# Packing two heads or row blocks into the TensorE array, folding one layer's weights, and fixing the issue order in three attention layers

## The chip, the cores and the metric

The kernel runs on one core of a Trainium2 chip. The metric is the device time of one execution in microseconds (us), median of several runs on the same chip. Each kernel is compared with runs of before from its own rounds. Where two changed kernels are compared below, their medians can come from different jobs and chips; before's median was 5836.9 to 5843.3 us there, so such differences are good to some 6 us.

## The reference, cut to what matters

Four layers follow each other on two images of 512 channels and 32 x 32 = 1024 pixels, all in fp32. Layer 0 (a deformable attention with a position bias, then an MLP) is the longest and is not changed. Layers 1 to 3 are attention over 1024 pixels:

```python
# layer 1: group norm, 8 heads of 64 channels, projection, residual
w = softmax(einsum('bct,bcs->bts', q * scale, k * scale));  hh = einsum('bts,bcs->bct', w, v)
x = x + proj_w @ hh
# layer 2: group norm, one head of 512 channels, projection, residual
attn = softmax(einsum('bci,bcj->bij', q, k) * C ** -0.5);   out = einsum('bcj,bij->bci', v, attn)
x = x + w_proj @ out
# layer 3: q and k have 64 channels, softmax over the queries, residual
attn = softmax(einsum('bdi,bdj->bij', q, k), axis=1);       x = gamma * einsum('bci,bij->bcj', v, attn) + x
```

## The kernel before

Every attention goes through one helper. It takes 128 rows of one head at a time: scores into PSUM, row maximum, exponential, division by the sum, eight transposes, two copies out of PSUM; after four such row blocks the values are multiplied. The emission order is only a proposal: the framework's scheduler sets the order of instructions on each engine.

```python
    def attend(qk, scale, vT, chunks, store):
        for tb in range(2):
            pT = [ptp.tile([P, 4, HALF], F32, name="pT", tag="pT") for _ in range(2)]
            for t4 in range(4):
                rows = slice(tb * HALF + t4 * P, tb * HALF + (t4 + 1) * P)
                sc = ps_s.tile([P, HW], F32, name="score")
                for half in range(2):
                    n = slice(half * HALF, (half + 1) * HALF)
                    for i, (q, k) in enumerate(qk):
                        nc.tensor.matmul(sc[:, n], q[:, rows], k[:, n], start=(i == 0), stop=(i == len(qk) - 1))
                nm = small.tile([P, 1], F32, name="nm")
                nc.vector.tensor_reduce(nm, sc, AX.X, ALU.max)
                nc.vector.tensor_scalar(nm, nm, -scale, None, ALU.mult)
                p = pp_.tile([P, HW], F32, name="p")
                sm = small.tile([P, 1], F32, name="den")
                nc.scalar.activation(p, sc, AF.Exp, bias=nm, scale=scale, accum_out=sm)
                nc.vector.reciprocal(sm, sm)
                nc.gpsimd.tensor_scalar(p, p, sm, 1.0, ALU.mult, ALU.mult)
                # ... eight transposes into two PSUM tiles tp; VectorE copies one to pT, ScalarE the other
            # ... values: for each chunk of channels, 8 matmuls of vT against pT, 512 columns wide

    for b in range(B):  # layer 1: eight heads of 64 channels
        # ... group norm, projections q, k, values vT
        for head in range(8):
            m, r = head // 2, slice(head % 2 * 64, head % 2 * 64 + 64)
            # ...
            attend([(q[m][r], k[m][r])], 64 ** -0.5, vT, [(head * 64, 64)], store)
        add_projection(x, proj1, "proj_b", o)
```

A score matmul of layer 1 uses 64 of the 128 rows of the TensorE array, a value matmul 64 of its 128 columns. PSUM holds two score tiles of two banks each, two `tp` tiles, and two tiles for all other products.

## Time and profile before

The median was 5840.04 us of three runs (5839.96 to 5842.33). The stages of the profiled run, from the first starts of their matmuls:

| stage | from (us) | to (us) | length |
|---|---|---|---|
| layer 0 with its MLP | 0 | 4182 | 4182 |
| layer 1, two images | 4182 | 5068 | 886 |
| layer 2, two images | 5068 | 5553 | 485 |
| layer 3, two images | 5553 | 5837 | 284 |

The page's first part gives each engine's busy time, its share of the span and its number of instructions:

```profile
PE 5147.2 (88%) x14146; PEld 1848.4 (32%) x14146; DVE 2487.8 (43%) x2868; ACT 1559.0 (27%) x1820; POOL 1469.3 (25%) x804
```

PE is TensorE, PEld its weight loads, DVE VectorE, ACT ScalarE, POOL GpSimd.

### The profile page before, as it was taken

To read this page: it belongs to the slowest core of one execution; us is meant where nothing else is said; L and a number is where in the kernel's file an instruction comes from. 1 tells how busy PE (TensorE), PEld (TensorE's weight loads), DVE (VectorE), ACT (ScalarE), POOL (GpSimd) and SP (SyncE) were. 2 spreads that over 40 slices of the span, in tenths; PEclk is the share of its full clock that TensorE was granted. 3 is DMA by queue.
4 is the path that set the end of the run, shared out by engine and by line. 5 is a ranking of instruction groups with operands and counts; after the bars stand their busy time and mean duration, and the time that the engine had idled before them with its cause. 6 is when DMAs were issued, how large, how long until landed. Compare 5 with 4: busy or idle time off the path is not lost.

```text
span 5837.3 us, 35881 instructions
## 1 busy us (share of the span) xinstructions
PE 5147.2 (88%) x14146; PEld 1848.4 (32%) x14146; DVE 2487.8 (43%) x2868; ACT 1559.0 (27%) x1820; POOL 1469.3 (25%) x804
## 2 busy tenths in 40 slices
PE   3788888888888888888888888899999999999999
PEld 1222222222222222222222222344444444444444
DVE  6455555555555455555555555200034334311121
ACT  3233333333333233333333333100123223210111
POOL 1233333333333233333333333100012112100000
PEclk7999999999999999999999999999989989999988
DMA  2100000000000000000000000000100000000000
GB/s 91 37 15 8 8 15 8 9 14 8 12 10 8 8 15 8 7 15 8 8 15 8 8 15 0 29 0 0 58 0 1 0 0 1 9 0 0 0 13 17
DMA packets 51416, 70.36 MB, mean 12 GB/s; under 512 B 7072, under 2 KB 40240, under 8 KB 50608
## 3 DMA queue, kind: packets, MB, share of 16 engines
q1 hardware_dynamic: 48992, 63.09, 4.1%
q10 hardware_dynamic: 2256, 4.98, 0.2%
q8 instruction: 112, 1.84, 0.1%
q14 instruction: 56, 0.46, 0.0%
HBM read 63.59 MB, written 4.46 MB: 12 GB/s over the span
## 4 chain that ended last, share of the span: by engine, by line
PE 62%; DVE 20%; ACT 9%; POOL 4%; DMA 4%; issue 2%; ACTq 0%; POOLq 0%; SPq 0%; DVEq 0%
PE z L318 18%; DVE h L320 9%; ACT h L314 8%; DVE h L307 8%; PE pav L531 8%; PE sim L325 7%; PE score L507 7%; PE pm L478 4%; PE ph L395 4%; PE pp L402 4%; DMA tab<-slog_d 3%; PE tp L520 3%; PE pmv L488 3%; POOL h L307 3%; PE ppr L542 2%
## 5 line engine op out<-in xcount | busy, mean ns | idle before, releaser
L318 PE MATMUL z<-h,cpb_w 128*128 128x512 f32 x4096 | 1983.0, 614 | 492.4 <-ACT h L314 492.4
L320 DVE TENSOR_SCALAR h<-z,pc 128x1024 f32<-128x1024 f32 x1024 | 1311.2, 1280 | 1549.4 <-PE z L318 1549.2
L314 ACT ACTIVATE h<-h 128x1024 f32<-128x1024 f32 x1024 | 1082.0, 1057 | 2363.1 <-DVE h L307 1852.2
L307 POOL TENSOR_TENSOR h<-tab,tab 128x1024 f32<-128x1024 f32 x512 | 1161.8, 2269 | 2090.9 <-PE z L318 2090.8
L318 PEld LDWEIGHTS z<-h,cpb_w 128*128 128x128 f32 x4096 | 696.6, 189 | 1806.2 <-ACT h L314 1106.9
L325 PE MATMUL sim<-h,w 128*32 128x512 f32 x4096 | 1033.1, 603 | 3.7 <-DVE h L320 3.7
L307 DVE TENSOR_TENSOR h<-tab,tab 128x1024 f32<-128x1024 f32 x512 | 625.3, 1221 | 13.9 <-POOL tab L299 13.9
L515 POOL TENSOR_SCALAR p<-p,den 128x1024 f32<-128x1024 f32 x160 | 178.7, 1117 | 1271.8 <-DVE den L514 1078.6
L531 PE MATMUL pav<-pT,vT 128*64 128x512 f32 (+1 forms) x1024 | 462.0, 609 | 0.2 <-DVE pT L525 0.2
L507 PE MATMUL score<-qk 64*128 64x512 f32 (+1 forms) x832 | 424.4, 655 | 7.4 <-ACT p L513 7.0
L325 PEld LDWEIGHTS sim<-h,w 128*32 128x32 f32 x4096 | 169.1, 108 | 748.0 <-issue 545.0
L509 DVE TENSOR_REDUCE nm<-score 128x1 f32<-128x1024 f32 x160 | 195.6, 1222 | 174.9 <-PE score L507 174.9
L531 PEld LDWEIGHTS pav<-pT,vT 128*64 128x64 f32 (+1 forms) x1024 | 169.1, 168 | 289.0 <-issue 286.1
L513 ACT ACTIVATE p<-score,nm 128x1024 f32<-128x1024 f32 x160 | 178.5, 1116 | 264.0 <-DVE nm L510 264.0
L520 PE MATMUL tp<-cst,p 128*128 128x128 f32 x1280 | 192.9, 299 | 33.1 <-POOL p L515 33.1
L395 PE MATMUL ph<-xn,wa 128*128 128x512 f32 x512 | 220.5, 592 | 1.1 <-POOL xn L388 1.1
L402 PE MATMUL pp<-hid,wb 128*128 128x512 f32 x512 | 220.4, 592 | 0.0
L523 ACT COPY pT<-tp 128x512 f32<-128x512 f32 x160 | 93.3, 583 | 451.0 <-PE tp L520 451.0
L520 PEld LDWEIGHTS tp<-cst,p 128*128 128x128 f32 x1280 | 152.1, 151 | 165.0 <-POOL p L515 93.9
L491 DVE TENSOR_TENSOR vT<-pmv,vbias 128x512 f32<-128x512 f32 x48 | 33.2, 691 | 398.5 <-PE pmv L488 398.5
L507 PEld LDWEIGHTS score<-qk 64*128 64x128 f32 (+1 forms) x832 | 145.4, 199 | 174.6 <-issue 137.6
L405 DVE SCALAR_TENSOR_TENSOR x<-pp,pc,x 128x512 f32<-128x512 f32 x16 | 12.0, 750 | 416.1 <-PE pp L402 416.1
(135 smaller groups left out, 2030.6 us busy)
## 6 DMA issues: line engine op xcount, KB each, us to landing
tab<-slog_d SPq DMA_DIRECT2D x64, 512.0 KB, 7.5
xt<-in_xt ACTq DMA_DIRECT2D x4, 1024.0 KB, 9.5
x<-in_x SPq DMA_DIRECT2D x8, 512.0 KB, 10.6
wa<-in_mlp_w SPq DMA_DIRECT2D x4, 1024.0 KB, 8.5
wb<-in_mlp_w SPq DMA_DIRECT2D x16, 256.0 KB, 5.3
out<-x SPq DMA_DIRECT2D x16, 256.0 KB, 2.0
wa<-in_qkv_w SPq DMA_DIRECT2D x4, 768.0 KB, 7.7
wb<-in_qkv_w SPq DMA_DIRECT2D x4, 768.0 KB, 6.4
```

The costliest lines, as they stand in the source:

```text
L307: eng.tensor_tensor(h1, tabs[0][:, quad, ri, :].unsqueeze(1).to_broadcast([P, H, W]), tabs[1][:, quad, ri, :].unsqueeze(2).to_broadcast([P ...
L314: nc.scalar.activation(h1f, h1f, AF.Relu)
L318: nc.tensor.matmul(z[:, n], cpb_w2, h1f[:, n], start=True, stop=True)
L320: nc.vector.tensor_scalar(h2, z, col("cpb_b2"), 0.0, ALU.add, ALU.max)
L325: nc.tensor.matmul(sim[quad * 32 : quad * 32 + 32, n], w3[:, 31 - r : 63 - r], h2s[quad][:, n], start=False, stop=(r == 31),)
L395: nc.tensor.matmul(ph, w1[:, k, m * P : (m + 1) * P], xn[:, k, :], start=(k == 0), stop=(k == CC - 1))
L402: nc.tensor.matmul(pp, w2[:, k, m * P : (m + 1) * P], h1[:, k, :], start=(k == 0), stop=(k == HID // P - 1))
L478: nc.tensor.matmul(pm[:rows], w[:, k, cols], h[k][:, n], start=(k == 0), stop=(k == CC - 1))
L507: nc.tensor.matmul(sc[:, n], q[:, rows], k[:, n], start=(i == 0), stop=(i == len(qk) - 1))
L509: nc.vector.tensor_reduce(nm, sc, AX.X, ALU.max)
L520: nc.tensor.transpose(tp[:, i, :], p[:, s * P : (s + 1) * P], ident)
L531: nc.tensor.matmul(pm[:n], vT[:, s, lo : lo + n], pT[s // 4][:, s % 4, :], start=(s == 0), stop=(s == 7))
```

## The change

The change wants TensorE to do less, and to fix the order by hand so that the packing holds:

- layer 1: two heads of a channel chunk share the array, in the scores by rows, in the values by columns; the values come in blocks of 256 rows;
- layer 2: `q'k = h' (Wq'Wk) h` and `Wproj (Wv h) = (Wproj Wv) h`, so two products of weights are made on chip once, and an image needs neither a key nor an output projection;
- layer 3: two row blocks share the array in the scores, and the projections of q and k are written twice side by side;
- everything after the MLP keeps the order of emission on each engine (`in_order`), with each pass's transposes and values one or two passes behind its scores, and projections and group norms cut into steps between them.

```diff
+@contextmanager
+def in_order(tc):
+    # ... collects the instructions emitted inside
+        if i.engine in before:
+            tc.add_manual_dep(i, before[i.engine], ..., reason="in_order")
+        before[i.engine] = i.name
...
+    def softmax(sc):
+        nm = small.tile([P, 1], F32, name="nm", tag="nm", bufs=4)
+        nc.vector.tensor_reduce(nm, sc, AX.X, ALU.max, negate=True)
+        p = pp_.tile([P, HW], F32, name="p")
+        sm = small.tile([P, 1], F32, name="den", tag="den", bufs=4)
+        nc.scalar.activation(p, sc, AF.Exp, bias=nm, accum_out=sm)
+        nc.vector.reciprocal(sm, sm)
+        nc.gpsimd.tensor_scalar(p, p, sm, 1.0, ALU.mult, ALU.mult)
+        return p
...
+    def scores1(qk, rb):
+        # ...
+        for half in range(2):
+            n = slice(half * HALF, (half + 1) * HALF)
+            for head in range(2):
+                r = slice(head * 64, head * 64 + 64)
+                nc.tensor.matmul(sc[head][:, n], q[r, rows], k[r, n], start=True, stop=True)
+        return [softmax(s) for s in sc]
...
+        for s in range(8):                       # values, weigh1
+            for head in range(2):
+                nc.tensor.matmul(pm[head * 64 : head * 64 + 64], vT[:, s, lo : lo + 64], pTs[head][:, s, :], ...)
...
+        for i in range(32):                      # layer 1, one image
+            m, rb = divmod(i, 8)
+            ps = scores1(qk, rb)
+            # ... on some passes one step of the next pair's projection, or of a group norm
+            # ... then the transposes of pass i - 1, both heads
+            if i % 2 and i >= 3:
+                weigh1(vT, o, (i - 3) // 8, (i - 3) // 2 % 4, block_T.pop((i - 3) // 2))
```

The diff is cut to its core; names and order are as in the kernel.

## The prediction

> **What bounds the kernel now.** I read the page first, then busy time by stretch, then the timeline, then single records. Layers 1 to 3 run from 4182 to 5837 us. The order of instructions on each engine is the same in both programs up to the end of the MLP (only one load is gone), so about 4182 us cannot move, and all is decided in 1655 us. The windows view (start and end, length, then busy time of each engine, and the granted clock) of layer 1's attention of one image, of layer 2's and of layer 3's:
>
> ```profile
> core 0: us, PE busy (x) PEld busy (x) DVE busy (x) ACT busy (x) POOL busy (x), PEclk, DMA share, GB/s
> 4273.00:4597.00 324.00, 312.82 (x1024) 133.40 (x1024) 142.54 (x273) 113.49 (x194) 71.52 (x64) 0.95 0.00 1
> 5160.00:5283.00 123.00, 118.77 (x319) 55.26 (x318) 23.07 (x40) 16.88 (x26) 8.93 (x8) 0.99 0.00 0
> 5595.00:5695.00 100.00, 94.98 (x229) 43.83 (x229) 22.96 (x41) 13.73 (x24) 8.94 (x8) 0.85 0.05 19
> ```
>
> TensorE is the bound in all three, at 95 to 97%, with VectorE below half. So fewer TensorE passes should help, as long as something else does not start to wait. The clock of 0.85 in layer 3 says that time is lost there in another way. The timeline shows both the packing and the clock:
>
> ```profile
> 2003.04 1.90 PE L325 MATMUL sim<-h,w 128*32 128x512 f32 x10
> ...
> 4300.77 3.78 PE L507 MATMUL score<-qk 64*128 64x512 f32 x4
> ...
> 4313.21 1.09 PE L520 MATMUL tp<-cst,p 128*128 128x128 f32 x8
> 4314.23 1.12 PE L507 MATMUL score<-qk 64*128 64x512 f32 x2
> 4316.31 1.13 PE L507 MATMUL score<-qk 64*128 64x512 f32 x4
> 4323.19 1.98 PE L507 MATMUL score<-qk 64*128 64x512 f32 x4
> ```
>
> An fp32 matmul is two records, 429 ns apart at 512 columns. Two score records take 1.12 us, and four on both halves of the rows take 1.13 us: two heads already share the array here by chance, while four alone take 1.98 us. The sim line does the same with column strips, ten records in 1.90 us. So packing works at nearly the full factor, for rows and for columns. At 4300 us the same four records take 3.78 us: the clock is at half from 4277 to 4308 us, although TensorE has no gap there.
>
> **What the skill says.** "TensorE: Matmul & The Clock Gate", Part 1, has a free-running activity window of 3413 ns after which the clock goes from full to half or back. The trace agrees: the records of the clock hold 0.5 for multiples of 3.41 us. From the starts of the matmuls I worked out each window's share of activity, counting a lone 64-row matmul as half. Over some 1,600 windows the clock fell only where the share was at most 0.36 and rose only where it was 0.75 or more. Part 4 of that page has transposes not counting as busy; here windows with 0.16 of scores and 0.50 of transposes kept the full clock, so I count them. "TensorEngine Tiling (Array Packing)", section PSUM Bottleneck, warns that packing speeds TensorE and not what empties PSUM. No stage before is limited so; this is where I expect it. The same page's Key Properties have a drain when the tiling mode changes: 520 ns to the next start where the form changes, against 429.
>
> **The change part by part.** Units: a 512-column fp32 matmul is 0.857 us, four plus four transposes 0.9 to 1.0 us.
>
> Layer 2: the keys' and the output's projection vanish, 32 + 32 matmuls an image, 2 x 64 x 0.857 = 110 us. In their place come 48 transposes and 32 matmuls once (some 10 + 27 us), 32 products with one column (about 8 us from the group norm's pairs of 0.39 us), and a wait of 8 us for layer 2's weights: they can be loaded only when the MLP has let go of the slot at 4181, and landed by 4191 before. So 54 us of it come back. The group norm goes beside matmuls, 2 x 8 us. Attention: scores 8 x 6.96, transposes 8 x 1.0, values 4 x 13.9 (256 columns, 214 ns each) = 119 us for 123 now, still TensorE bound. A layer 2 image costs 27 + 27 + 119 = 174 instead of 243 us.
>
> Layer 1: packed scores save half of 256 matmuls in two images, packed values another half of 256: 256 x 0.857 = 219 us of TensorE work. Will it be time? One pass of the loop takes two heads' 128 rows. The durations of its chain, from the page:
>
> ```profile
> L509 DVE TENSOR_REDUCE nm<-score 128x1 f32<-128x1024 f32 x160 | 195.6, 1222 | 174.9 <-PE score L507 174.9
> L513 ACT ACTIVATE p<-score,nm 128x1024 f32<-128x1024 f32 x160 | 178.5, 1116 | 264.0 <-DVE nm L510 264.0
> L525 DVE COPY pT<-tp 128x512 f32<-128x512 f32 x160 | 109.7, 685 | 85.4 <-PE tp L520 84.1
> L523 ACT COPY pT<-tp 128x512 f32<-128x512 f32 x160 | 93.3, 583 | 451.0 <-PE tp L520 451.0
> ```
>
> The fixed order makes VectorE do: maximum of head A, reciprocal A, maximum B, reciprocal B, then the two copies of the rows before. The built program shows exactly this. A reciprocal waits for its exponential, so VectorE stands still twice. From the first score: scores 1.98; hop 0.09; then twice maximum 1.22, hop 0.12, exponential to reciprocal 1.24 (median of the records), reciprocal 0.1: 7.4 us; copy 0.7: 8.1. The second head's eight transposes need the two PSUM buffers that this copy and ScalarE's empty, so they run 8.2 to 9.2. Only then come the values (every second pass, 16 packed pairs of 214 ns, 3.6 us with the switches) and the next scores. Even passes 9.2, odd 12.8: 22.0 us a pair, while TensorE's own work is some 14. An image has 16 pairs: 352, less 6 for the first pair, plus 12 for group norm work that sits on VectorE inside this chain: 358 us against 324 now. The next pair's projections (24 of the 32 steps an image) hide in the waits, 3.4 us each.
>
> The clock: in an odd pass TensorE idles from 2.8 to 8.2 us. A hole of 5.4 us holds a window below 0.35 at any phase, so the clock halves, and the second head's transposes and the values start cold. Depending on phase it comes back 3 to 6 us after work resumes, half of which is lost: 2.1 us. A projection shortens the hole to about 2 us, a share of 0.38, just safe. Without projection are four of eight passes for three head pairs and all eight of the last: (3 x 4 + 8) x 2.1 = 43 us an image. So the attention loop is 401 us for an image where it was 324.
>
> Layer 3: scores packed, but the same chain: first pass 7.4, then three of 9.2 + 13.9, last 2.3 + 13.9, cold starts about 8: 101 us, and 41 for projections and values: 143 an image against 142.
>
> Sum in us from the start: MLP end 4182; fold 54, first q and k 14, values 27: 4277; image 0 401, next image's q and k sticking out 9, tail 6: 4693; values and projection 55: 4748; image 1 401, layer 2's product 27, tail 4: 5180; values and projection 55: 5235; layer 2 174 + 120: 5529; layer 3 286: 5815; last store and launch edges some 6: 5821. I say 5825.
>
> **Rivals.** First, packing pays in full: if VectorE's chain hid behind TensorE, layer 1 loses 219, layer 2 some 70 net, and the time is about 5550. For it speaks that TensorE was 97% busy and VectorE 44% in the layer 1 stretch; against it the fixed order, in which nothing of VectorE's can move ahead of a reciprocal that waits. Second, the chain holds but the clock stays up (packed matmuls counting more, or the hole being shorter): 2 x 43 + 2 x 8 less, about 5720. Third, the clock also falls in the passes with a projection, whose share of 0.38 is close to 0.36: 24 passes of up to 2.1 us, and longer cold stretches feed on themselves: 5870 to 5920. Fourth, matmuls of 256 columns might wait for their weights (190 ns a load against 214 ns of streaming): at 20 ns each over the some 1,000 such records of layers 2 and 3, 20 us more.
>
> **Range and chances.** The part outside layer 1 is arithmetic on measured durations, good to 20 us. The chain is good to 0.5 us in 64 passes, 32 us; the clock's share may be 0 to twice 100. That gives 5740 to 5915. Under 5723 needs the chain and the clock both milder than reckoned, over 5957 needs cold passes nearly throughout; that such a rewrite is meant to gain adds a little to faster.
>
> **What would show it.** After: in layer 1 a stretch of loop near 400 us an image, TensorE busy about 75%, waits of the transposes on VectorE's or ScalarE's copies as TensorE's longest, the maximum's idle time ended by reciprocals and exponentials, the eight score records of a pass in about 2 us, mean clock near 0.85 there and near 1 in layer 2, each layer 2 loop near 120 us. I am wrong if the loop takes under 330 us, if the waits of the transposes are short, or if packed pairs run one after the other.

## More of the kernel before

What counts for the change is what TensorE waits for inside layer 1's attention. The waits of TensorE, from 4273 to 4597 us (who waited for whom: us in total, times, longest):

```profile
PE tp L520 <- POOL p L515: 8.4, 9, 3.3
PE score L507 <- ACT p L513: 2.4, 1, 2.4
```

These are 11 of 324 us: the scheduler had interleaved the heads so well that TensorE almost never stood still.

## The result, and the profile after

The changed kernel takes 5818.28 us (5813.74 to 5821.17, four runs) against 5840.0 of before: a ratio of 0.9963, 95% interval 0.9949 to 0.9977. Ratios are the mean time of one kernel's fast runs over that of the other's of the same rounds, so they are not quite the ratios of the medians quoted. The results are correct. The page has TensorE busy 247 us less:

```profile
PE 4900.4 (84%) x15154; PEld 1930.7 (33%) x15154; DVE 2459.4 (42%) x2736; ACT 1571.5 (27%) x1848; POOL 1472.3 (25%) x804
```

The stages against the prediction's sum, in the profiled run of 5819 us:

| stage | before | predicted | measured |
|---|---|---|---|
| end of the MLP to the first layer 1 score | 91 | 95 | 109 |
| layer 1 loop, image 0, with what sticks out | 324 | 416 | 408 |
| layer 1 loop, image 1, with layer 2's first product | 323 | 432 | 425 |
| layer 2, image 0, with the next image's products | 243 | 174 | 182 |
| layer 2, image 1 | 242 | 120 | 118 |
| layer 3, two images | 284 | 286 | 285 |

The columns do not cut the work in the same places (projections moved into the loops), so the first column shows only the scale. The windows view of the changed kernel, for layer 1's loop of image 0, layer 2's loop of image 1 and layer 3's of image 0; the columns are those of the prediction's first fence:

```profile
4291.00:4699.00 408.00, 293.89 (x1412) 164.54 (x1412) 141.97 (x234) 125.81 (x213) 76.54 (x68) 0.83 0.00 1
...
5417.00:5534.00 117.00, 116.65 (x446) 79.03 (x445) 23.12 (x39) 13.98 (x25) 8.97 (x8) 1.00 0.00 0
5576.00:5675.00 99.00, 81.94 (x352) 64.29 (x352) 30.50 (x54) 14.59 (x25) 8.97 (x8) 0.88 0.06 21
```

In layer 1 TensorE is now busy 294 of 408 us, 72% where it was 97%, and at a mean clock of 0.83. Layer 2's loop of image 1 has no holes. A pass is the work on one block of 128 rows of two heads; each head pair has eight. The timeline of TensorE for two passes of layer 1, the second cut, after the values of the pass before:

```profile
4377.99 3.67 PE L647 MATMUL pav<-pT,vT 128*64 128x256 f32 x32
4381.60 1.99 PE L638 MATMUL score<-k,q 64*128 64x512 f32 x8
4383.51 1.09 PE L544 MATMUL tp<-cst,p 128*128 128x128 f32 x8
4389.40 1.94 PE L544 MATMUL tp<-cst,p 128*128 128x128 f32 x8 [4.79 <-ACT pT L547]
4391.26 3.79 PE L638 MATMUL score<-k,q 64*128 64x512 f32 x8
...
4400.86 1.94 PE L544 MATMUL tp<-cst,p 128*128 128x128 f32 x8 [4.49 <-ACT pT L547]
4402.73 5.21 PE L647 MATMUL pav<-pT,vT 128*64 128x256 f32 x32
```

The eight score records of two heads take 1.99 us, as four of one head did before, and 32 value records 3.67 us: the packing works. But the second eight transposes of a pass wait 4.5 to 4.8 us for a copy, and what follows such a hole runs at half clock: transposes 1.94 instead of 1.09, scores 3.79 instead of 1.99, values 5.21 instead of 3.67. VectorE in the pass that starts at 4381.60 shows where the wait comes from:

```profile
4383.61 1.23 DVE L530 TENSOR_REDUCE nm<-score 128x1 f32<-128x1024 f32 x1 [1.42 <-PE score L638]
4386.17 0.16 DVE L534 RECIPROCAL den<-den 128x1 f32<-128x1 f32 x1 [1.33 <-ACT p L533]
4386.25 1.22 DVE L530 TENSOR_REDUCE nm<-score 128x1 f32<-128x1024 f32 x1
4388.81 0.16 DVE L534 RECIPROCAL den<-den 128x1 f32<-128x1 f32 x1 [1.33 <-ACT p L533]
4388.89 0.67 DVE L549 COPY pT<-tp 128x512 f32<-128x512 f32 x1
```

Both reciprocals end a stop of 1.33 us in which VectorE waits for an exponential. The transposed rows of the first head have lain in PSUM since 4384.6, and the copy that frees a buffer starts at 4388.89. ScalarE's copy stands behind the second exponential, and so behind the same reciprocal; in this pass it freed the first buffer, and most of the waiting ends with it. TensorE's waits in the same loop:

```profile
PE tp L544 <- ACT pT L547: 74.8, 16, 6.3
PE tp L544 <- DVE pT L549: 24.6, 17, 1.9
```

The transposes wait 99 us for copies where before they waited 8.4 us for GpSimd. A hole also costs through the clock, which the next section takes apart.

### The profile page after: what moved, and what is told of

Its sections match the earlier page's. It is cut to its first block, busy times and chain, and to the rows that moved or that the text cites. A ratio compares the mean times of both kernels' runs of the same rounds, so it can differ in the third digit from the quotient of the medians.

```text
span 5819.4 us, 37975 instructions
## 1 busy us (share of the span) xinstructions
PE 4900.4 (84%) x15154; PEld 1930.7 (33%) x15154; DVE 2459.4 (42%) x2736; ACT 1571.5 (27%) x1848; POOL 1472.3 (25%) x804
## 4 chain that ended last, share of the span: by engine, by line
PE 55%; DVE 20%; ACT 11%; POOL 5%; DMA 3%; issue 2%; ACTq 0%; POOLq 0%; SPq 0%; DVEq 0%
PE z L337 18%; DVE h L339 9%; ACT h L333 8%; DVE h L326 8%; PE sim L344 7%; PE pav L505 4%; PE ph L415 4%; PE pp L422 4%; DMA tab<-slog_d 3%; PE pmv L505 3%; POOL h L326 3%; PE pav L647 3%; PE score L638 3%; ACT p L533 2%; PE tp L544 2%
## 5 line engine op out<-in xcount | busy, mean ns | idle before, releaser
L544 PE MATMUL tp<-cst,p 128*128 128x128 f32 x1280 | 219.2, 326 | 241.1 <-ACT pT L547 180.5
L544 PEld LDWEIGHTS tp<-cst,p 128*128 128x128 f32 x1280 | 178.5, 169 | 319.4 <-issue 280.6
L505 PE MATMUL pav<-pT,vT 128*128 128x256 f32 x1024 | 233.5, 390 | 1.5 <-DVE pT L549 1.5
L505 PEld LDWEIGHTS pav<-pT,vT 128*128 128x128 f32 x1024 | 199.6, 196 | 32.5 <-DVE pT L549 3.7
L638 PE MATMUL score<-k,q 64*128 64x512 f32 x512 | 154.4, 714 | 8.5 <-ACT p L533 8.5
L549 DVE COPY pT<-tp 128x512 f32<-128x512 f32 x160 | 108.4, 681 | 108.1 <-PE tp L544 107.5
L647 PE MATMUL pav<-pT,vT 128*64 128x256 f32 x1024 | 150.4, 458 | 0.0
```

Source lines behind the costliest of these rows:

```text
L505: nc.tensor.matmul(pm, w, m, start=(k == 0), stop=(k == len(pairs) - 1))
L544: nc.tensor.transpose(tp[:, i, :], p[:, s * P : (s + 1) * P], ident)
L638: nc.tensor.matmul(sc[head][:, n], q[r, rows], k[r, n], start=True, stop=True)
L647: nc.tensor.matmul(pm[head * 64 : head * 64 + 64], vT[:, s, lo : lo + 64], pTs[head][:, s, :], start=(s == 0), stop=(s == 7),)
```

## The experiments

The theory: the fixed order makes a pass of layer 1 as long as VectorE's chain, and the clock falls in the hole that this leaves on TensorE. The rivals: TensorE's work is still what counts; the packing is worth less than it seems; the clock does not matter. All experiments gave correct results; each was run three rounds against before.

**Late reciprocals.** In layers 1 and 3 the maxima of both heads come first, the reciprocals after the copies.

```diff
-        return [softmax(s) for s in sc]
+        return [softmax_a(s) for s in sc]        # maximum, exponential
...
                 for head in range(2):
                     transposed(...)
+                for s_ in ps:
+                    softmax_b(*s_)                # reciprocal, division
```

> In layers 1 and 3 the two maxima come first on VectorE, then the copies of the transposed rows, and only then the two reciprocals; no work is added or removed. If VectorE's fixed order with its two stops at the exponentials sets the length of a pass (my theory), the second head's transposes can start 1.7 us earlier: a pair of passes goes from 22.0 to about 18.8 us, 32 pairs give 100 us, some 40 us of cold clock and 15 us of layer 3 go with it: about 5660 us (5630 to 5700). If TensorE's own work or the packing is what holds (rival), nothing changes: 5818 within 15 us.

Measured: 5645.33 us, ratio 0.967 (0.9655 to 0.9684). Moving the two reciprocals of a pass, 0.16 us each, and the divisions on GpSimd behind them, without adding or removing work, gave 173 us; in the profiled runs 153 us of it lie between layer 1's first score and layer 2's, and 24 in layer 3. VectorE in a pass of layer 1:

```profile
4369.79 2.35 DVE L530 TENSOR_REDUCE nm<-score 128x1 f32<-128x1024 f32 x2 [3.65 <-PE score L647]
4372.06 0.68 DVE L558 COPY pT<-tp 128x512 f32<-128x512 f32 x1
4373.55 0.69 DVE L558 COPY pT<-tp 128x512 f32<-128x512 f32 x1 [0.81 <-PE tp L553]
4374.16 0.21 DVE L538 RECIPROCAL den<-den 128x1 f32<-128x1 f32 x2
```

The first copy starts 2.3 us after the first maximum, where it was 5.3 us. Passes without values went from 9.1 to 7.9 us. The order of VectorE was what set the pass; the rival falls.

**Serial scores.** The loops over heads and halves are exchanged, so that one head's scores are issued before the other's.

```diff
-        for half in range(2):
-            # ... n of this half
-            for head in range(2):
+        for head in range(2):
+            # ... r of this head
+            for half in range(2):
                 # ...
                 nc.tensor.matmul(sc[head][:, n], q[r, rows], k[r, n], start=True, stop=True)
```

> In layer 1 the scores of the two heads are no longer issued alternately but one head after the other, so they cannot share the array: 64 passes, each with 1.71 us more of TensorE time. If the pass is set by VectorE's chain (my theory), this hides in the hole of TensorE: within 25 us of the changed kernel, 5800 to 5845 us, and the clock falls less often, as the hole is shorter. If packing the scores is worth its TensorE time (rival), 64 x 1.71 = 110 us are lost: about 5925 us.

Measured: 5813.86 us, ratio 0.9959 (0.9944 to 0.9974), as the theory expected, but the run proves nothing. Its timeline shows that the scores stayed packed:

```profile
4408.36 1.99 PE L638 MATMUL score<-k,q 64*128 64x512 f32 x8
```

The built program has two matmuls of one head and then two of the other; in the trace the eight records start in four pairs, 13 or 14 ns apart. Taken in the program's order, the second head's first record could not start before the first head's fourth, over 1.2 us later.

**Filling with matmuls.** Four matmuls into a spare PSUM tile that nobody reads, in every layer 1 pass that has no projection step.

```diff
+            if (m == 3 or rb in (0, 1, 3, 5)) and not (b == 0 and i == 31):
+                fill()      # 4 matmuls of 512 columns
```

> Four 512-column matmuls of 3.4 us, whose result nobody reads, are put into the hole of every layer 1 pass that has no projection in it, 46 passes in two images, some 158 us of pure waste on TensorE. If the hole is idle anyway and costs twice because the clock falls in it (my theory), the clock in layer 1 stays at 1 and the kernel gets faster by up to 86 us: 5730 to 5770 us. If the clock does not matter (first rival), it stays at 5818 within 10 us. If TensorE's work bounds layer 1 (second rival), it goes up to 5975 us.

Measured: 5756.6 us, ratio 0.9863 (0.9846 to 0.9879). The text on record miscounts: it is 39 passes, not 46 (20 of 32 in each image, less one), so the waste is 39 x 3.43 = 134 us of TensorE time. Adding it made the kernel 62 us faster than the changed one. So TensorE's work is not what counts, since its time in the hole is free, and the rival that the clock does not matter falls too: work was only added, and the clock is what rose, as the next run's windows show.

**Filling with transposes.** The same with 32 transposes.

```diff
-        accumulate(pm, [(v2[:, k, :P], v2[:, k, :]) for k in range(CC)])
+        for k in range(32):
+            nc.tensor.transpose(pm[:, k % 4, :], v2[:, k % 4, k // 8 * P : k // 8 * P + P], ident)
```

> The same filling as in the run with matmuls, but with 32 transposes of 0.109 us, 3.5 us. If transposes count as activity for the clock, as I read the trace of before, the result is that of the matmuls: 5730 to 5770 us and a layer 1 clock near 1. If they do not count, as the skill says, the clock falls just as without filling, and the time stays at 5818 or goes up by the cold transposes (32 at half clock take 7 us and would stick out by some 2 us in each of 46 passes): 5818 to 5910 us.

Measured: 5762.06 us, ratio 0.9871 (0.9856 to 0.9885), the same as with matmuls. The windows view from 4291 to 4650 us of the run with matmuls, then of the run with transposes:

```profile
4291.00:4650.00 359.00, 305.33 (x1448) 160.07 (x1447) 137.59 (x228) 121.28 (x206) 76.33 (x68) 0.96 0.00 1
```

```profile
4291.00:4650.00 359.00, 302.75 (x1874) 196.05 (x1874) 136.61 (x227) 118.99 (x203) 75.66 (x68) 0.96 0.00 1
```

Both hold the clock at 0.96 where it was 0.83. Transposes, fp32 ones, count as activity here, against Part 4 of the Trainium skill's "TensorE: Matmul & The Clock Gate".

**Early values.** One statement moves: the values of an older block come before the transposes of the last pass.

```diff
+            if i % 2 and i >= 3:
+                weigh1(...)
             if len(pend) == 2:
                 # ... transposes of pass i - 1
-            if i % 2 and i >= 3:
-                weigh1(...)
```

> Only one line moves: in layer 1 the values of the block before are issued ahead of the transposes instead of after them. If the odd pass is long because the values stand behind transposes that wait for VectorE (my theory), they now fill the hole: odd passes go from 12.7 to 14.8 us down to 9.2, 30 x 3.6 = 108 us plus some 50 us of cold clock: about 5660 us (5630 to 5700). If TensorE's work is what counts (rival), the same work in another order gives 5818 within 15 us.

Measured: 5680.25 us, ratio 0.9725 (0.9711 to 0.974). Counting a head pair's passes from 0, passes 3 and 5, which have values and no projection step, went from 14.8 to 9.0 us: 3.6 us of values fit into the hole, and the clock no longer falls there.

**Free order.** The line that fixes the order is taken out; the packing, the folding and the emission stay.

```diff
-    post.enter_context(in_order(tc))
```

> The fixed order is taken away: the scheduler may move instructions, and in the built program it puts both maxima before the reciprocals, but also splits packed pairs (one score matmul, eight transposes, three score matmuls). If VectorE's order is what costs (my theory), this is faster than the changed kernel although packing is spoiled: 5620 to 5740 us. If the fixed order is what makes the packing pay, as the change intends (rival), it is slower than 5818: 5860 to 5950 us.

Measured: 5533.26 us, ratio 0.9482 (0.9461 to 0.9503), faster than I expected and 285 us faster than the changed kernel. The edit frees all engines and all that follows the MLP: by the profiled runs some 245 us of the gain lie between layer 1's first score and layer 2's, 22 in layer 3, and the rest at the start and in layer 2. The scheduler puts both maxima before the reciprocals and spreads values and transposes over the holes. The same loop of layer 1, image 0, here from 4280 to 4565 us:

```profile
4280.00:4565.00 285.00, 273.93 (x1416) 145.66 (x1413) 135.67 (x222) 124.89 (x213) 76.26 (x68) 0.99 0.00 1
```

TensorE is back at 96% and the clock at 0.99. The rival, that the fixed order is what makes the packing pay, falls: this fixed order ate the gain. The scheduler does split packed scores in every second pass, as expected:

```profile
4415.76 1.12 PE L637 MATMUL score<-k,q 64*128 64x512 f32 x2 [1.58 <-ACT p L532]
4416.82 1.09 PE L543 MATMUL tp<-cst,p 128*128 128x128 f32 x8
4417.84 1.98 PE L637 MATMUL score<-k,q 64*128 64x512 f32 x6
```

These eight score records take 3.1 us instead of 1.99. A free order in which they stay together was not tried.

**Both edits.** Late reciprocals and early values.

> Late reciprocals and early values together: an even pass 7.4 to 8.1 us, an odd one 7.9, a pair 15.7 instead of 22.0 at full clock, and holes only in passes without a projection or values. 31 pairs x 6.3 = 195, clock some 60, layer 3 some 25: about 5540 us (5510 to 5590). If the two edits remove the same wait (rival), the gain is that of the better one alone, about 5645 us.

Measured: 5566.67 us, ratio 0.9531 (0.9516 to 0.9545). The gain over the changed kernel is 252 us; the single edits gave 173 and 138. So they share some 60 us, but the rival of one and the same wait falls. In the first three head pairs of an image most passes take 7.9 or 8.0 us, of which TensorE is busy all but some 0.4.

**Serial scores with both edits.**

> The run with both edits, but with layer 1's scores one head after the other again. In the changed kernel this cost nothing (5814 against 5818). If packing is worth its TensorE time only once the chain is out of the way (my theory), it now costs 0.9 to 1.7 us in each of 64 passes: 60 to 110 us over the run with both. If row packing is worth nothing in itself (rival), it stays within 15 us of that run.

Measured: 5567.57 us, ratio 0.953 (0.9514 to 0.9546). By its expectation the rival would have won. But here too the trace has the eight score records in 1.99 us, so nothing was undone.

**Walled scores.** One transpose that nobody reads stands between the two heads' scores, so that the array is needed whole in between; first in the changed kernel, then in the one with both edits.

```diff
         for head in range(2):
+            if head:
+                wall = ps_m.tile([P, P], F32, name="wall", tag="mm")
+                nc.tensor.transpose(wall, v2[:, 0, :P], ident)
             for half in range(2):
```

> The run with serial scores did not undo the packing: its trace has the eight score records of a pass still in 1.99 us, side by side. Here one transpose of the full array, whose result nobody reads, stands between the two heads' scores, so they take about 4.0 us. If the chain of VectorE sets the pass (my theory), 64 x 2.1 = 134 us of TensorE time hide almost wholly, 20 us stick out where a projection fills the hole: 5800 to 5850 us. If packed scores are worth their time here (rival), 5930 to 5955 us.

> The same wall in the kernel with late reciprocals and early values, where TensorE has little slack in an odd pass (7.9 us, of which 7.5 are work) and some in an even one with a projection. If packing pays once the chain is out of the way (my theory), about 2 us are lost in some 56 of 64 passes: 5640 to 5690 us against 5567. If packing the scores is worth nothing even there (rival), 5567 within 15 us.

The timeline of TensorE in the first of the two shows that the packing is gone, 4.15 us for what took 1.99:

```profile
4425.55 1.98 PE L641 MATMUL score<-k,q 64*128 64x512 f32 x4
4427.46 0.33 PE L637 MATMUL wall<-cst,v 128*128 128x128 f32 x1
4427.72 1.98 PE L641 MATMUL score<-k,q 64*128 64x512 f32 x4
```

Measured: 5856.9 us, ratio 1.0028 (1.0013 to 1.0043), in the changed kernel, and 5705.79 us, ratio 0.9764 (0.9747 to 0.9781), with both edits. The wall costs TensorE 64 x 2.16 = 138 us. Of the 2.16 us, 1.71 are the packing (before, eight score records of one head took 3.70) and some 0.45 the wall itself. In the changed kernel 39 us of the 138 show, a little above the expected range. They do not all hide behind VectorE's chain: passes 3 and 5 of a head pair even went from 14.8 to 14.0 us, and their shorter hole may have spared them cold clock, which was not tested apart. With both edits 139 us show, more than I expected: most passes of the first three head pairs went from 7.9 or 8.0 to 10.1 or 10.2 us, so there was no slack left in them. In the last head pair the clock has a part in it as well, in passes that went from 10.7 to 15.1 us while the wall costs 2.16. So packing the scores is worth little in the changed kernel and, less the wall itself, an estimated 64 x 1.71 = 110 us once VectorE's chain is out of the way.

**Two best versions.** Both edits, the projection's steps on passes 0, 2, 4 and 6 instead of 2, 4, 6 and 7, layer 3's values one pass later, layer 1's first q and k before layer 2's product of weights; once in a fixed order with a short filling in the last head pair, once with a free order and no filling.

```diff
+        # ... the first q and k before the product of the weights
+        drain(fold())
...
+                advance(qk_steps)          # a projection step on pass 0 of a head pair
...
+            # ... layer 3: scores of i; values of block i - 2; transposes of i - 1; reciprocals of i
```

> The best fixed order I can write from these findings: late reciprocals, early values, the projection's steps spread over the even passes, a short filling in the last head pair's even passes, layer 3's values one pass later, and layer 1's first q and k ahead of the product of layer 2's weights. From the 5567 us of both edits: layer 3 gives 34, the start 10, the spread steps and the clock 20: 5490 to 5525 us. If layer 3 and the start are bound by TensorE already (rival), 5540 to 5570.

> The same edits, except the filling, with the scheduler free to move instructions. It moved most of these things by itself in the run with a free order (5533 us), so I expect 5500 to 5535 us, no better than the fixed order. If the scheduler adds its own gain on top (rival), under 5490 us.

Measured: 5533.46 us, ratio 0.9473 (0.9459 to 0.9487), fixed, and 5518.64 us, ratio 0.9449 (0.9433 to 0.9465), free. The fixed one missed its range. Its layer 3 gave 9 us of the expected 34 (251 against 261 us in the run with both edits), and the start took 118 us from the MLP's end to the first score of layer 1, 7 more than in that run, for a reason told in the next section. The free one, 300 us faster than the changed kernel and 5.5% faster than before, is the best version found. It was expected to be no better than the fixed one and is 15 us faster, with no overlap of their runs; as it lacks the filling too, the order alone is not shown to be the cause. It splits the packed scores in nearly every pass.

## Why the prediction was right

**The sum.** 5825 was predicted, 5818 measured, within the range, and each stage of the table lies within 14 us of its prediction. The errors partly cancel: the start took 14 us more, layer 1's loops 15 us less. Two slips in the text change nothing: the 24 of 32 projection steps are those of two images, not of one, and (3 x 4 + 8) x 2.1 is 42.

**Layer 1's chain.** The step said passes of 9.2 and 12.8 us. The trace has 9.1 us for even passes with a projection and 12.7 for the odd passes that have one too, which keep the clock. Late reciprocals show that VectorE's order is the cause, early values that the place of the values adds to it. It is a chain of order and not of work: with the order free, a loop of the same instructions over image 0 takes 285 us instead of 408.

**The clock.** The step found 2.1 us lost in an odd pass without a projection, and took them for every pass without one. Passes 3 and 5 of a head pair do take 14.8 us, 2.1 more than 12.7. But pass 0 takes 9.7, only 0.6 more than 9.1, and pass 1, which follows it without a projection between, 16.5, 3.8 more: its scores run at half clock already. Together a head pair loses 8.6 us where the step has 4 x 2.1. So the sum was right and its spread over the passes was not, which is partly luck. Over all, filling the holes gave 62 us while the step's sum for layer 1 is 86. The fillings are not quite free, as some stick out, so the two do not contradict each other, but the 86 itself is not shown. The reading behind it held in the new trace: from 4190 us on the clock fell only in windows with an activity of 0.31 or less (46 of them) and stayed where it was 0.36 or more (326); it rose at 0.78 or more (47) and stayed down at 0.76 or less (57). This activity is worked out from the starts and widths of the matmuls, with transposes counted and a lone 64-row matmul as half. Were transposes left out, some windows that kept the full clock would come out at under 0.01.

**The fold.** The step had 54 us; the product of the weights ended at 4247.6, over 65 us after the 4182 of the sum. This is the step's largest miss. One term was missing and one too small. A tiny scaling of a bias stands in front of the group norm in VectorE's fixed order, and its 1536 numbers are loaded behind four megabytes of weights. VectorE after the MLP:

```profile
4193.89 0.23 DVE L451 TENSOR_SCALAR gb<-vb,pc 128x4 f32<-128x4 f32 x1 [12.59 <-DMA vb<-in_vb]
```

So the group norm starts 12.6 us late, and TensorE, whose own order has the group norm's matmuls between the weights' transposes, stands still for 7.2 us. This is also why the early q and k of the best fixed version gave nothing: they need the group norm, and TensorE waited 19.8 us for it there. And the 32 second products with one column took 6.96 us for the first ones' 4.60, and the clock had fallen, from 4238.6 us on by its records; by the reckoning of activity above, one column each leaves the array mostly idle. The step had about 8 us for both; they took 11.4.

**Layer 2.** 182 and 118 us for 174 and 120. The group norm was to lie beside matmuls. In image 0 it does not wholly: its own small matmul, and after it transposes, waited 3.0 and 2.3 us for VectorE, and the clock fell twice for 3.4 us. This was seen in the trace and not tested.

**Layer 3.** 285 for 286: packed scores and the chain cancel, as the step said.

**The rivals.** The first, 5550 us if the chain hid behind TensorE, is close to what the free order does (5533), which also gains some 21 us in layer 3 (263 for 284) that the rival did not count. The fixed order is what kept it from coming true. The second, a clock that stays up, described at 5720, is not what happened; the third, the clock falling also in passes with a projection, neither, as those kept 9.1 us, but for one in the first head pair of each image (10.9 and 10.5). The fourth, slow value matmuls of 256 columns, neither: layer 2's second loop took 118 us.

## What to carry to other kernels

When an engine at 97% is relieved, ask before anything else what the next chain is, and write it down instruction by instruction in the order in which each engine will meet it: here a reciprocal in front of a copy, in a strict order, cost 173 us, most of the 219 us of TensorE's work that packing saves. Fix an order only around waits that have been measured, or leave it to the scheduler and compare; and issue work that is ready ahead of work that waits. A hole on TensorE costs twice when it is long enough for the clock to fall, and even useless matmuls or transposes in it can pay, here 62 and 56 us.

## What the Trainium skill lacked or had wrong

- "TensorE: Matmul & The Clock Gate", Part 4, has transposes not keeping the clock up. Here, in fp32, 32 of them in a hole held layer 1's clock at 0.96, as four matmuls did, against 0.83 without.
- The same page gives the clock's window but no level of activity at which it falls or rises. In this trace it fell at 0.31 or less and rose at 0.78 or more of a window, a lone 64-row matmul counted as half; in the trace of before it fell at 0.36 or less and rose at 0.75 or more.
- The same page, Part 3, has matmuls starting in strict program order. With one head's two fp32 score matmuls ahead of the other's in the built program, the first records of the two still started 13 ns apart, and eight records took 1.99 us. Compiled again, the run's kernel file has this order in TensorE's finished instruction stream too, four matmul instructions on one half of the rows and then four on the other, so it is after the compiler that they change places. One full-width transpose between them ends it (4.15 us).
- "TensorEngine Tiling (Array Packing)" warns of PSUM evacuation after packing, which was right in kind. What it lacks is that the order on the evacuating engines decides: with the same copies, 5818 us in the fixed order and 5533 in the scheduler's.
